# A four-layer attention and expert kernel: routing of the second mixture in one step, gate weights in the rows, loads ordered behind reads

## The chip, the core and the metric

One core of one Trainium2 chip runs the whole kernel: TensorE (matmuls and transposes), VectorE, ScalarE, GpSimd (here also the indirect DMAs) and the DMA queues, SP's above all. The metric is the device time in microseconds (us) of one execution, median of several runs.

## The reference, cut to what matters

The input is x of 4 batches x 512 tokens x 128 columns, and a context of 32 rows a batch. Four layers follow one another, each an attention over the context and a feed-forward part, both added to x. The change is in the feed-forward part of the third layer (layer index 2, "the second mixture": 8 experts, the two best for each token, 640 places per expert) and in the start of the fourth layer, whose feed-forward part is again a mixture of experts.

```python
def _moe_forward(x, w_g, c_fc, c_proj):
    ...
    logits = xf @ w_g
    topv, topi = jax.lax.top_k(logits, TOP_K)
    full = full.at[jnp.arange(N)[:, None], topi].set(topv)
    probs = jax.nn.softmax(full, axis=-1)
    ...
    rank = jnp.cumsum(mask.reshape(TOP_K * N, N_EXP), axis=0).reshape(TOP_K, N, N_EXP) - 1
    mask = mask * (rank < capacity)
    ...
    exp_batches = jnp.einsum('nec,nd->ecd', sec_mask, xf)
    h = jax.nn.gelu(jnp.einsum('ecd,edh->ech', exp_batches, c_fc), approximate=False)
    exp_out = jnp.einsum('ech,ehd->ecd', h, c_proj)
    out = jnp.einsum('nec,ecd->nd', cb, exp_out)
```

All first choices come before all second choices in an expert's count; a token whose rank is over the capacity is dropped there. With two choices the softmax weights are w1 = 1 / (1 + exp(m2 - m1)) for the larger logit m1, and w2 = w1 * exp(m2 - m1).

## The kernel before, in words

Tokens lie on 128 partitions; a batch is a tile X[g] of 128 x 4 x 128 f32, and all work is done batch by batch. Each batch's work is a Python generator, a chain; `together` traces the chains in turns, one step (up to the next `yield`) of each per turn, and chain g begins two turns after chain g - 1. The framework plans the order of instructions on each engine from that: what was traced earlier goes first among what it takes to be ready by its own costs, so that work of several batches is interleaved on an engine, but each engine then executes its queue strictly in this order and waits where an operand is late. Semaphores are set by the framework.

**Attention and normalisation.** `moments` makes the statistics (L203 to L216, with Ln and Exp on ScalarE at L208 and L209), `normed` the normalised tile (L230 on ScalarE or L234 on VectorE), `transposed` four TensorE transposes (L244) and a copy (L246). `psum(fill=5)` puts five matmuls of the identity on TensorE first (L93, "fillers"), whose results nobody reads. `attend` is the attention proper (L396 scores, L381 to L383 softmax, L409 transposes, L415 values), `proj` the projection (L256), `add_to` the addition to X (L468). `attend_few` is the attention with few keys of layers 1 and 2 (L441, L457, L463).

**Second mixture, routing.** After layer 2's attention, `routed` (tag 2) normalises into the tiles rows[g] (128 x 4 x 129: the row and the number of its token) and makes the logits (matmuls L575, copy L581). `dispatch.chain(g)` then has three steps. First the two best experts of each token (twice L633 to L639 on VectorE, with L642 between), and the counts per expert (matmul L649, copy to SBUF L651). Second the ranks: matmuls L654 to L657 with this and the earlier batches' counts, then L660 to L672 on VectorE, which end in `to`, the row of each choice in the DRAM table xs2; its tiles have two buffers (`own`). Third, 8 scatters (L680), each an indirect DMA issued by GpSimd that writes 128 rows; those of first choices wait for the landing of the earlier batches' second choices. `finish` makes `back` (L712), which marks the places of each expert that hold second choices, and the weights wt[0] and wt[1] for all tokens (L715 to L719). `l3_weights` (L319, L338 and others) prepares the next layer's keys after that.

**Second mixture, experts.** `l2_ffn` reads each expert's 640 rows (L1147, three experts ahead), and takes them in two groups, of 3 x 128 and of 2 x 128: transposes (L835), copy (L836), first product (L1171), Gelu on ScalarE (L1174), second product (L1179), copy of the results from PSUM (L1186), and a scatter per 128 results to the DRAM table yd2 (L1188); its row numbers are made per expert at L1164. `combine(g)` reads both results of each token of a batch (L1204, two reads of 256 KB) and adds them to X with their weights (L1210, eight operations per batch).

**Fourth layer.** Per batch: `combine2`, `attend3` (`normed`, `transposed` with 5 fillers, `attend`, GpSimd's addition of a bias at L1235, `proj`), `route3` (`routed` with 5 fillers). Beside these four chains a fifth, `fetch`, traces the loads of the last mixture's weights f3w1 and f3w2 (L1407, L1408; 1 MB each) from turn 8 on. Their tiles use the space of the second mixture's weights, and can be loaded when the last product that reads those is done. `l3_ffn` is the last mixture (L1253, L1254, L1301, L1311), which runs all experts for all tokens.

Reads, loads and the stores of the output are all on SP's queue.

Of the kernel before, what the change touches and what calls it, by code (L numbers as in the profile page):

```python
# [8 lines left out]
F32 = mybir.dt.float32  # L9
# [7 lines left out]
P = 128  # L17
D = 128
B = 4
# [52 lines left out]
def tile_kernel(ctx: ExitStack, tc: tile.TileContext, I, out):  # L72
# [489 lines left out]
    def routed(tag, w, bias=None, copies=(), fill=0, rows=None):  # L562
# [5 lines left out]
        def chain(g):  # L568
# [3 lines left out]
            xnT[g] = yield from transposed(xn[g], fill=fill)  # L572
# [35 lines left out]
    def dispatch(dp, C2, xs, cleared, rows, logits, wt):  # L608
# [9 lines left out]
        m = dp.tile([P, 2, NT], F32, tag="m", name="m")  # L618
# [4 lines left out]
        def own(cols, name, dtype=F32):  # L623
            return dp.tile([P] + cols, dtype, tag=name, name=name, bufs=2)

        def chain(g):
# [4 lines left out]
            w = own([2, n], "w")  # L631
            for k in range(2):
                nc.vector.tensor_reduce(m[:, k, ts], L, AX.X, ALU.max)  # L633
                at = own([n, NEXP], "at", BF16)
                nc.vector.tensor_tensor(at, L, bc(m[:, k, ts], 2, NEXP), ALU.is_equal)
# [9 lines left out]
            while len(counts) < g:  # L645
                yield
# [5 lines left out]
            yield  # L652
# [22 lines left out]
            yield  # L675
# [29 lines left out]
        def finish():  # L705
# [7 lines left out]

            d = dp.tile([P, NT], F32, tag="d", name="d")
            nc.vector.tensor_tensor(d, m[:, 1], m[:, 0], ALU.subtract)  # L715
            nc.scalar.activation(d, d, AF.Exp)
            nc.vector.tensor_scalar(wt[0], d, 1.0, None, ALU.add)
            nc.vector.reciprocal(wt[0], wt[0])
            nc.vector.tensor_tensor(wt[1], wt[0], d, ALU.mult)  # L719
            return back  # L720
# [412 lines left out]
    def l2_ffn(xs, yd, back, wt, f2w1, f2w2, meanwhile):  # L1133
        made = []

# [8 lines left out]
        def read(e):  # L1144

            xg.append(ex.tile([P, NCH2, D + 1], F32, tag="xg", name="xg", bufs=4))
            nc.sync.dma_start(xg[e], xs[e * L2_CAP : (e + 1) * L2_CAP].rearrange("(p c) d -> p c d", c=NCH2))  # L1147
# [10 lines left out]
        for i, (e, c0, m) in enumerate(groups):  # L1158
            if c0 == 0:
# [4 lines left out]
                nc.vector.scalar_tensor_tensor(to, back[:, e, :], float(NTOK), xg[e][:, :, D], ALU.mult, ALU.add)  # L1164
            if i + 1 < len(groups):
# [20 lines left out]
            nc.vector.tensor_copy(flat(y[:, :m, :]), pt[:, : m * D])  # L1186
# [11 lines left out]

        def combine(g):
            ys = []  # L1200
            for k, tag in enumerate(("o", "oT")):
                y = wk.tile([P, NJ, D], F32, tag=tag, name="yg", bufs=B)
                at = k * NTOK + g * S
                nc.sync.dma_start(y, yd[at : at + S].rearrange("(j p) d -> p j d", p=P))  # L1204
                ys.append(y)
            yield
            for j in range(NJ):
                for k in range(2):
                    xj = X[g][:, j, :]
                    nc.vector.scalar_tensor_tensor(  # L1210
# [412 lines left out]
```

## Time and profile before

| | us |
|---|---|
| timed, median of 3 runs | 660.22 (657.69 to 662.02) |
| profiled execution | 654.48 |
| its span, first to last instruction | 652.7 |
| TensorE busy | 533.0 (82% of the span) |
| VectorE busy | 330.6 (51%) |
| ScalarE busy | 238.9 (37%) |
| GpSimd busy | 152.6 (23%) |

From the page: the span in 40 slices of 16.3 us, each digit the busy share in tenths; PEclk is TensorE's granted clock in tenths of full speed, DMA the mean busy share of the 16 DMA engines.

```profile
PE   2569889735988888899663799991899999999996
...
DVE  4686554663278532789742211213877863233232
...
POOL 4243233335302102000476155541200000000000
PEclk9887999956989999999867799996699999999999
DMA  9960001221495009200011321018000000000000
```

Slices 19 to 22 (counted from 0; 310 to 375 us) hold the second mixture's routing and scatters: POOL is at 4 to 7 there, and TensorE falls to 3 before it. In slices 23 to 26 the experts run on a full TensorE. Slice 27 (440 to 457 us) is the gap between the second mixture's last product and the fourth layer: TensorE at 1, the DMA engines at 8. From slice 32 on the last mixture keeps TensorE full to the end. Busy time of an instruction is that of the instruction alone; overlapped matmuls count more than the time they take.

### The profile page before, as it was taken

What the parts mean: (1) busy time and instruction counts of PE and PEld (TensorE: products, weight loads), DVE (VectorE), ACT (ScalarE), POOL (GpSimd) and SP (SyncE); (2) the same over time, 40 slices, a digit from 0 to 9 for tenths busy, and PEclk for the clock granted to TensorE, in tenths of its full rate; (3) what the DMA queues carried; (4) which work ended last, traced back from release to release, by engine and by line L of the source; (5) the groups of instructions that cost most, each with busy time, mean ns of one, the idle gap of its engine ahead of it and who ended that gap; (6) DMA issues with size and microseconds to landing.
All of it is one profiled execution on the core that took longest, in us unless ns stands there. A gap on an engine that the chain in (4) does not pass through costs nothing.

```text
span 652.7 us, 9532 instructions
## 1 busy us (share of the span) xinstructions
PE 533.0 (82%) x3426; PEld 423.4 (65%) x3426; DVE 330.6 (51%) x1361; ACT 238.9 (37%) x539; POOL 152.6 (23%) x188
## 2 busy tenths in 40 slices
PE   2569889735988888899663799991899999999996
PEld 2558667525986655798541688880578866767664
DVE  4686554663278532789742211213877863233232
ACT  2353655411227621542210233340555343333432
POOL 4243233335302102000476155541200000000000
PEclk9887999956989999999867799996699999999999
DMA  9960001221495009200011321018000000000000
GB/s 321 312 210 17 18 17 50 64 81 38 158 305 211 1 1 314 81 2 2 29 49 53 106 78 61 32 34 271 3 0 2 1 1 2 17 0 17 7 11 17
DMA packets 41985, 48.84 MB, mean 75 GB/s; under 512 B 5129, under 2 KB 29074, under 8 KB 41762
## 3 DMA queue, kind: packets, MB, share of 16 engines
q1 hardware_dynamic: 38690, 40.56, 18.9%
q0 software_dynamic: 2816, 5.79, 2.7%
q10 hardware_dynamic: 432, 1.89, 0.8%
q8 instruction: 27, 0.44, 0.3%
q14 instruction: 20, 0.16, 0.1%
HBM read 37.72 MB, written 13.14 MB: 78 GB/s over the span
## 4 chain that ended last, share of the span: by engine, by line
PE 47%; POOL 8%; issue 7%; DMA 6%; DVE 5%; ACT 4%; SPq 1%; DVEq 0%; POOLq 0%; ACTq 0%
PE pt L1301 9%; PE pt L1253 9%; POOL yd L1188 6%; PE pt L93 5%; PE pt L396 3%; PE po L415 3%; PE pt L244 3%; PE pt L256 2%; DMA yd<-ye,to 2%; PE pt L1045 2%; PE pt L575 2%; DMA e_wg<-in_e_wg 1%; ACT xnT L246 1%; PE pt L409 1%; PE pt L983 1%
## 5 line engine op out<-in xcount | busy, mean ns | idle before, releaser
L1301 PEld LDWEIGHTS pt<-f3w,hT 128*128 128x128 f32 x512 | 65.3, 191 | 33.2 <-ACT hT L1254 19.4
L1311 DVE SCALAR_TENSOR_TENSOR x<-pt,gates,x 128x128 f32<-128x128 f32 x128 | 35.9, 344 | 76.6 <-PE pt L1301 76.5
L1254 ACT ACTIVATE hT<-pt,cols 128x512 f32<-128x512 f32 x64 | 44.0, 687 | 73.5 <-PE pt L1253 73.0
L1301 PE MATMUL pt<-f3w,hT 128*128 128x128 f32 x512 | 68.5, 277 | 1.0 <-ACT hT L1254 0.6
L1253 PE MATMUL pt<-xnT,f3w 128*128 128x512 f32 x128 | 65.1, 597 | 0.0
L93 PE MATMUL pt<-cst 128*128 128x128 f32 x392 | 55.4, 289 | 0.0
L93 PEld LDWEIGHTS pt<-cst 128*128 128x128 f32 x392 | 51.2, 204 | 2.8 <-issue 1.5
L1188 POOL DMA_INDIRECT yd<-ye,to x40 | 38.3, 957 | 48.8 <-DVE ye L1186 25.4
L680 POOL DMA_INDIRECT xs<-rows,to x32 | 31.0, 968 | 64.4 <-issue 61.0
L1174 ACT ACTIVATE hT<-pt 128x384 f32<-128x384 f32 (+1 forms) x64 | 27.6, 437 | 45.5 <-PE pt L1171 43.9
L246 ACT COPY xnT<-pt 128x512 f32<-128x512 f32 x40 | 23.4, 584 | 55.9 <-PE pt L244 55.6
L203 DVE BATCH_NORM_STATS2 st<-x 128x6 f32<-128x128 f32 x128 | 32.4, 271 | 22.0 <-POOL x L556 16.1
L1179 PEld LDWEIGHTS pt<-f2w,hT 128*128 128x128 f32 x320 | 39.6, 191 | 3.3
L1179 PE MATMUL pt<-f2w,hT 128*128 128x128 f32 x320 | 40.6, 279 | 0.0
L244 PE MATMUL pt<-cst,xn 128*128 128x128 f32 x80 | 18.2, 324 | 25.6 <-ACT xn L230 18.4
L1171 PE MATMUL pt<-exT,f2w 128*128 128x256 f32 (+1 forms) x128 | 38.9, 447 | 0.2 <-DVE exT L836 0.2
L1186 DVE COPY ye<-pt 128x384 f32<-128x384 f32 (+1 forms) x16 | 7.9, 491 | 51.8 <-PE pt L1179 51.8
L244 PEld LDWEIGHTS pt<-cst,xn 128*128 128x128 f32 x80 | 12.0, 159 | 32.2 <-ACT xn L230 21.2
L1171 PEld LDWEIGHTS pt<-exT,f2w 128*128 128x128 f32 x128 | 23.8, 197 | 8.9 <-issue 1.4
L381 DVE TENSOR_REDUCE mx<-pt 128x16 f32<-128x512 f32 (+1 forms) x32 | 22.0, 687 | 14.4 <-PE pt L396 13.9
L396 PE MATMUL pt<-keys,xnT 128*128 128x256 f32 (+1 forms) x64 | 27.6, 540 | 1.3 <-ACT xnT L246 1.3
L415 PEld LDWEIGHTS po<-v,aT 128*128 128x128 f32 x192 | 24.8, 199 | 4.9 <-issue 3.5
(330 smaller groups left out, 1053.5 us busy)
## 6 DMA issues: line engine op xcount, KB each, us to landing
e_w<-in_e_w SPq DMA_DIRECT2D x8, 512.0 KB, 6.4
e_wg<-in_e_wg SPq DMA_DIRECT2D x8, 512.0 KB, 6.8
yg<-yd SPq DMA_DIRECT2D x12, 256.0 KB, 4.2
xs<-in_empty SPq DMA_DIRECT2D x1, 2580.0 KB, 11.3
xg<-xs SPq DMA_DIRECT2D x8, 322.5 KB, 3.0
f0w<-in_f_w SPq DMA_DIRECT2D x1, 2048.0 KB, 13.5
yd<-zero SPq DMA_DIRECT2D x8, 256.0 KB, 3.7
ew<-in_e_w SPq DMA_DIRECT2D x8, 256.0 KB, 4.1
```

The source lines that it names most:

```text
L93: nc.tensor.matmul(pt[:, :P], lhsT=ident, rhs=ident, start=True, stop=True)
L203: nc.vector.bn_stats(st[:p, j, :], src[:, j, :])
L244: nc.tensor.transpose(pt[:, j * P : (j + 1) * P], src[:, j, :], ident)
L396: nc.tensor.matmul(pt[:, j * nk : (j + 1) * nk], lhsT=xT[:, (j0 + j) * P : (j0 + j + 1) * P], rhs=keys, start=True, stop=True,)
L415: nc.tensor.matmul(po[:, k, :], lhsT=aT[:, k * P : (k + 1) * P], rhs=of(values[k % nch], cols + hpc, g), start=True, stop=True,)
L1171: nc.tensor.matmul(pt[:, : m * P], lhsT=f2w1[:, e, f * P : (f + 1) * P], rhs=xT, start=True, stop=True)
L1179: nc.tensor.matmul(pt[:, c * D : (c + 1) * D], lhsT=hT[:, f, c * P : (c + 1) * P], rhs=f2w2[:, e, f, :], start=f == 0, stop=f == 3,)
L1188: ins = nc.gpsimd.indirect_dma_start(out=yd[:], out_offset=bass.IndirectOffsetOnAxis(ap=to[:, c0 + c : c0 + c + 1], axis=0), in_=y[:, c, : ...
L1253: nc.tensor.matmul(pt, lhsT=f3w1[:, e, f * P : (f + 1) * P], rhs=xnT[g], start=True, stop=True)
L1254: nc.scalar.activation(hT[:, f, :], pt, AF.Gelu, bias=col["f3_b1"][:, 2 * e + f : 2 * e + f + 1])
L1301: nc.tensor.matmul(pt[:, j, :], lhsT=hT[:, f, j * P : (j + 1) * P], rhs=f3w2[:, e, f, :], start=f == 0, stop=f == 1,)
L1311: nc.vector.scalar_tensor_tensor(xj, pt[:, j, :], ge, xj, ALU.mult, ALU.add)
```

## The change

The routing of the second mixture (`dispatch.chain`) becomes one step: the `yield`s after the counts and after the ranks go, and the waiting loop ahead of the counts becomes an assertion. Its small tiles get four buffers in place of two.

The weights are computed in that step per batch, between the counts and the ranks, and put into two more columns of the rows (128 x 4 x 131), so that they travel with the scatter; the DRAM table, the table of empty rows and the experts' input tiles are wider by two columns. `finish` loses the weights and makes `first` = 1 - `back` in addition. In `l2_ffn` three small operations per expert make `gate`, the weight that belongs to each place, and the copy of the results from PSUM becomes a multiplication by it. `combine` then adds two whole tiles per batch.

The fillers go from `route2` (all batches), from `attend3` (all but batch 0) and from `route3` (all but batch 3).

`fetch` waits (in tracing) until the combining reads of all batches are traced, and its two loads get a dependency on the landing of all eight reads.

```diff
@@ routed @@
-            xnT[g] = yield from transposed(xn[g], fill=fill)
+            xnT[g] = yield from transposed(xn[g], fill=fill[g] if isinstance(fill, tuple) else fill)
@@ dispatch @@
-        m = dp.tile([P, 2, NT], F32, tag="m", name="m")
...
         def own(cols, name, dtype=F32):
-            return dp.tile([P] + cols, dtype, tag=name, name=name, bufs=2)
+            return dp.tile([P] + cols, dtype, tag=name, name=name, bufs=B)
...
+            m = own([2, n], "m")
             for k in range(2):
-                nc.vector.tensor_reduce(m[:, k, ts], L, AX.X, ALU.max)
+                nc.vector.tensor_reduce(m[:, k], L, AX.X, ALU.max)
...
             nc.scalar.copy(ohs[:, 2], ohs[:, 0])
-            while len(counts) < g:
-                yield
+            assert len(counts) == g
...
             nc.scalar.copy(cs[: 2 * width], pt[: 2 * width, :P])
-            yield
+
+            d = own([n], "d")
+            nc.vector.tensor_tensor(d, m[:, 1], m[:, 0], ALU.subtract)
+            nc.scalar.activation(d, d, AF.Exp)
+            w1, w2 = rows[g][:, :, D + 1], rows[g][:, :, D + 2]
+            one = own([n], "one")
+            nc.vector.tensor_scalar(one, d, 1.0, None, ALU.add)
+            nc.vector.reciprocal(w1, one)
+            nc.vector.tensor_tensor(w2, w1, d, ALU.mult)
             pt = psum()[:, : 3 * width]
             nc.tensor.matmul(pt, lhsT=tri, rhs=flat3, start=True, stop=False)
...
                     to[:, k], at[:, k], float(NSLOT + (L2_CAP if k else -1)), over[:, k], ALU.add, ALU.max
                 )
-            yield
...
         def finish():
...
-            d = dp.tile([P, NT], F32, tag="d", name="d")
-            nc.vector.tensor_tensor(d, m[:, 1], m[:, 0], ALU.subtract)
-            nc.scalar.activation(d, d, AF.Exp)
-            nc.vector.tensor_scalar(wt[0], d, 1.0, None, ALU.add)
-            nc.vector.reciprocal(wt[0], wt[0])
-            nc.vector.tensor_tensor(wt[1], wt[0], d, ALU.mult)
-            return back
+            first = rk.tile([P, NEXP, NCH2], F32, tag="first", name="first")
+            nc.vector.tensor_scalar(first, back, -1.0, 1.0, ALU.mult, ALU.add)
+            return back, first
@@ l2_ffn @@
-            xg.append(ex.tile([P, NCH2, D + 1], F32, tag="xg", name="xg", bufs=4))
+            xg.append(ex.tile([P, NCH2, D + 3], F32, tag="xg", name="xg", bufs=4))
...
                 nc.vector.scalar_tensor_tensor(to, back[:, e, :], float(NTOK), xg[e][:, :, D], ALU.mult, ALU.add)
+
+                gate = ex.tile([P, NCH2, 2], F32, tag="gate", name="gate", bufs=4)
+                nc.vector.tensor_tensor(gate[:, :, 1], back[:, e, :], xg[e][:, :, D + 2], ALU.mult)
+                nc.vector.tensor_tensor(gate[:, :, 0], first[:, e, :], xg[e][:, :, D + 1], ALU.mult)
+                nc.vector.tensor_tensor(gate[:, :, 0], gate[:, :, 0], gate[:, :, 1], ALU.add)
...
-            nc.vector.tensor_copy(flat(y[:, :m, :]), pt[:, : m * D])
+            nc.vector.tensor_tensor(
+                y[:, :m, :], pt[:, : m * D].rearrange("p (c d) -> p c d", d=D), bc(gate[:, c0 : c0 + m, 0], 2, D), ALU.mult
+            )
...
+        combined = []
+
         def combine(g):
...
-                nc.sync.dma_start(y, yd[at : at + S].rearrange("(j p) d -> p j d", p=P))
+                combined.append(nc.sync.dma_start(y, yd[at : at + S].rearrange("(j p) d -> p j d", p=P)).ins)
                 ys.append(y)
             yield
-            for j in range(NJ):
-                for k in range(2):
-                    xj = X[g][:, j, :]
-                    nc.vector.scalar_tensor_tensor(
-                        xj, ys[k][:, j, :], wt[k][:, g * NJ + j : g * NJ + j + 1], xj, ALU.mult, ALU.add
-                    )
-            yield
+            for y in ys:
+                nc.vector.tensor_tensor(flat(X[g]), flat(y), flat(X[g]), ALU.add)
+            yield
@@ l3_xattn @@
-            xT = yield from transposed(x1, fill=5)
+            xT = yield from transposed(x1, fill=0 if g else 5)
@@ tile_kernel @@
-            route2, _, _, L = routed(2, wide["w_g"], None, (), 5, rows)
+            route2, _, _, L = routed(2, wide["w_g"], None, (), 0, rows)
...
-        route3, _, xnT, L = routed(3, wide["router"], fill=5)
+        route3, _, xnT, L = routed(3, wide["router"], fill=(0, 0, 0, 5))
...
             def fetch():
-                nc.sync.dma_start(f3w1, I["f3_w1"].rearrange("e d f -> d e f"))
-                nc.sync.dma_start(f3w2, I["f3_w2"].rearrange("e (c p) d -> p e c d", p=P))
+                while len(combined2) < 2 * B:
+                    yield
+                for load in (
+                    nc.sync.dma_start(f3w1, I["f3_w1"].rearrange("e d f -> d e f")).ins,
+                    nc.sync.dma_start(f3w2, I["f3_w2"].rearrange("e (c p) d -> p e c d", p=P)).ins,
+                ):
+                    for read in combined2:
+                        tc.add_manual_dep(
+                            load,
+                            read.name,
+                            mybir.DependencyInfo(mybir.DependencyClass.Sync, mybir.DependencyReason.DATA),
+                            reason="what is wanted now comes first",
+                        )
                 yield
```

More of the change, by code (lines that the diff above doesn't have):

```diff
@@ L606, in without, with dispatch @@
         return L2
-    def dispatch(dp, C2, xs, cleared, rows, logits, wt):
+    def dispatch(dp, C2, xs, cleared, rows, logits):
         same3, before3 = (dp.tile([P, 96], BF16, tag=n, name=n) for n in ("b_same3", "b_before3"))
@@ L631, in chain @@
             w = own([2, n], "w")
+            m = own([2, n], "m")
             for k in range(2):
-                nc.vector.tensor_reduce(m[:, k, ts], L, AX.X, ALU.max)
+                nc.vector.tensor_reduce(m[:, k], L, AX.X, ALU.max)
                 at = own([n, NEXP], "at", BF16)
-                nc.vector.tensor_tensor(at, L, bc(m[:, k, ts], 2, NEXP), ALU.is_equal)
+                nc.vector.tensor_tensor(at, L, bc(m[:, k], 2, NEXP), ALU.is_equal)
                 nc.vector.tensor_tensor(at, at, bc(rev, 1, n), ALU.mult)
@@ L1130, in l2_xattn, with l2_ffn @@
         return chain
-    def l2_ffn(xs, yd, back, wt, f2w1, f2w2, meanwhile):
+    def l2_ffn(xs, yd, back, f2w1, f2w2, meanwhile):
         made = []
+        back, first = back
         def ready(steps):
@@ L1203, in combine @@
                 at = k * NTOK + g * S
-                nc.sync.dma_start(y, yd[at : at + S].rearrange("(j p) d -> p j d", p=P))
+                combined.append(nc.sync.dma_start(y, yd[at : at + S].rearrange("(j p) d -> p j d", p=P)).ins)
                 ys.append(y)
             yield
-            for j in range(NJ):
-                for k in range(2):
-                    xj = X[g][:, j, :]
-                    nc.vector.scalar_tensor_tensor(
-                        xj, ys[k][:, j, :], wt[k][:, g * NJ + j : g * NJ + j + 1], xj, ALU.mult, ALU.add
-                    )
+            for y in ys:
+                nc.vector.tensor_tensor(flat(X[g]), flat(y), flat(X[g]), ALU.add)
             yield
-        return combine, made[0]
+        return combine, combined, made[0]
     def l3_weights():
@@ L1323, in tile_kernel @@
     yd2 = dram.tile([2 * NTOK + NEXP * L2_CAP, D], F32, tag="yd2", name="yd2")
-    xs2 = dram.tile([SPARE + 2 * NTOK, D + 1], F32, tag="xs2", name="xs2")
+    xs2 = dram.tile([SPARE + 2 * NTOK, D + 3], F32, tag="xs2", name="xs2")
     zero = wk.tile([P, NJ, D], F32, tag="oT", name="zero", bufs=B)
@@ L1375, in tile_kernel @@
         attend1, attend2 = l1_xattn(*made["few1"]), l2_xattn(*made["few2"])
-        wt = [rk.tile([P, NT], F32, tag=f"wt{k}", name=f"wt{k}") for k in range(2)]
         dp_scope = ExitStack()
@@ L1382, in l2_start @@
             C2 = packed("cst2", _CST2, pool=dp)
-            rows = [dp.tile([P, NJ, D + 1], F32, tag=f"rows{g}", name="rows") for g in range(B)]
-            route2, _, _, L = routed(2, wide["w_g"], None, (), 5, rows)
-            send, finish = dispatch(dp, C2, xs2, cleared2, rows, L, wt)
+            rows = [dp.tile([P, NJ, D + 3], F32, tag=f"rows{g}", name="rows") for g in range(B)]
+            route2, _, _, L = routed(2, wide["w_g"], None, (), 0, rows)
+            send, finish = dispatch(dp, C2, xs2, cleared2, rows, L)
             sent.append(finish)
@@ L1398, in tile_kernel @@
         with tc.tile_pool(name="ex2", bufs=1) as ex:
-            combine2, many3 = l2_ffn(xs2, yd2, back2, wt, f2w1, f2w2, l3_weights)
+            combine2, combined2, many3 = l2_ffn(xs2, yd2, back2, f2w1, f2w2, l3_weights)
         attend3 = l3_xattn(*many3)
@@ L1487, in _empty_slots @@
     import numpy as np
-    t = np.zeros((NSLOT, D + 1), np.float32)
+    t = np.zeros((NSLOT, D + 3), np.float32)
     t[:, D] = NTOK + np.arange(NSLOT)
```

## The prediction

> **What bounds the kernel now.** I read the page's slices first, then the chain of waits, then the timelines of the stretches that the change touches, and last the busy times in windows. The second mixture's routing, its experts and the results' way into the third stage lie between 300 and 525 us; before and after them the diff changes nothing but a table that is 1.6% larger.
>
> The timeline of GpSimd (start, duration, engine, line, operation, then in brackets the idle time before):
>
> ```profile
> 261.41 0.62 POOL L266 TENSOR_TENSOR keys<-kc,cst 128x256 f32<-128x256 f32 x1 [0.17 <-PE pt L1099]
> 316.95 1.02 POOL L680 DMA_INDIRECT xs<-rows,to  x1 [54.93 <-issue]
> 318.28 0.96 POOL L680 DMA_INDIRECT xs<-rows,to  x1 [0.30 <-DVE logits L642]
> ...
> 355.17 0.96 POOL L680 DMA_INDIRECT xs<-rows,to  x1 [0.30 <-issue]
> 356.44 0.96 POOL L680 DMA_INDIRECT xs<-rows,to  x1 [0.30 <-issue]
> ```
>
> From 316.95 the 32 scatters run back to back, 1.264 us apart: 40.45 us. GpSimd is the bound there, and only the start of the first scatter can move the end. Its timeline, all engines, shows what the first one waits for:
>
> ```profile
> 310.73 0.24 PE L649 MATMUL pt<-b_ones,ohs 128*64 128x128 bf16 x1 [2.29 <-DVE ohs L639]
> 310.90 1.42 PE L93 MATMUL pt<-cst 128*128 128x128 f32 x10
> 311.01 0.26 ACT L651 CAST cs<-pt 64x128 bf16<-64x128 f32 x1
> ...
> 314.67 0.29 PE L654 MATMUL pt<-ohs,b_tri 128*128 128x96 bf16 x1
> ...
> 316.04 0.24 DVE L672 SCALAR_TENSOR_TENSOR to<-row,over 128x4 int32<-128x4 f32 x2
> ```
>
> Batch 0's counts are in SBUF at 311.27, but its rank product (load at 314.46) stands behind other batches' matmuls, five fillers (L93) among them.
>
> From 363.5 to 441.2 TensorE is busy 77.64 of 77.7 us: the experts are TensorE-bound. Then the chain of waits (start, length):
>
> ```profile
> 443.53 4.99 DMA yd<-ye,to
> 448.54 2.61 DMA yg<-yd
> 452.23 1.13 DVE x L1210 x4
> 457.60 1.65 PE pt L244 x4
> 459.90 2.08 PE pt L396 x2
> 461.98 2.13 PE pt L93 x10
> ```
>
> The last scatter takes 4.99 us to land, where the median is 2.2. The two f3w loads are issued at 439.38 and 441.29 and take 5.4 and 7.1 us: all 16 DMA engines are at 0.86 to 0.93 from 440 to 448. Busy times by stretch (length, then PE, PEld, DVE, ACT, POOL, clock):
>
> ```profile
> 457.60:468.50 10.90, 9.02 (x26) 5.91 (x27) 10.21 (x45) 5.72 (x15) 2.76 (x2) 0.50 0.00 0
> 468.50:508.40 39.90, 39.14 (x258) 30.53 (x257) 29.80 (x83) 22.34 (x45) 2.54 (x2) 0.99 0.01 1
> 508.40:525.40 17.00, 15.28 (x127) 14.05 (x126) 12.44 (x63) 6.46 (x15) 0.00 (x0) 1.00 0.00 0
> ```
>
> First VectorE is full, with TensorE at half clock; then TensorE is full; in the tail both are nearly so.
>
> **Part 1, the routing.** With the three steps in one, the rank product is traced ahead of the other batches' steps, so it can follow the counts: 314.46 - 311.27 = 3.2 us less. On GpSimd the scatters pass nothing, for it idles from 262 to 317. The filler of batch 0 (chain: 303.53, 1.12 us) is in front of all this on a full TensorE: 1.1 us less. Added ahead of the scatter are d, Exp, one, reciprocal and w2: nearest rows L715 to L719 (0.22, 0.21, 0.18, 0.25, 0.17, on 16 columns, here 4), 1.0 us if all in line, nothing if they fit the 0.6 us in which the counts go to ScalarE and back. I take 0.4, since Exp is queued behind the counts' copy on ScalarE and VectorE, in order, then waits for it; behind that wait are batch 0's ranks and batch 1's normalisation. That normalisation (L234, 1.11 us) is traced earlier, and may push in between: 0 to 1.1, I take 0.4. First scatter: 3.2 + 1.1 - 0.8 = 3.5 us earlier (1.1 if the matmuls in between stay, 4.3 if all additions hide), at 313.4. Batch 1's index must then be there at 313.4 + 10.1 - 0.7 = 322.8. It was ready at 323.67, behind two fillers (1.12 and 1.34) and a late L654, so about 321: GpSimd is not starved, with 2 us to spare; batches 2 and 3 (331.86 and 339.43) have over 1 and 3 us even unmoved. Everything to 443.5 moves by 3.5. Four index buffers for two remove VectorE's 1.17 us wait at L672; GpSimd ends last anyway, so nothing. Rows of 524 instead of 516 bytes: 1.6% of a 2.80 us read, 0.04 us; of the 11.3 us table copy 0.2 us, unused until 317.
>
> **Part 2, the experts.** Eight times three gate operations of 0.17 us (L1164's row) are 4.1 us on VectorE, busy 14.5 of 77.7 us; TensorE's queue covers them. Uncovered they would cost those 4.1. At expert 0 they fall in the 0.76 us in which VectorE waits for the transposes. The eviction turns from a copy (558 ns for 384 columns) into a product with a broadcast operand: L382's row, 688 ns for 512, gives 516. Nothing. The finish loses five small operations and gains one (L712: 0.19), all under the scatters.
>
> **Part 3, the last loads behind the results.** Without the loads the last scatter should land in the usual 2.2 to 2.3 us: 4.99 - 2.3 = 2.7 us less (0 if its lateness is its own, 2.8 at best). The loads then go out on SP's queue once the eighth read has landed, some 9 us after the first read's issue. 2 MB at the 300 GB/s of this stretch is 7 us; L1253 needs them 74 us after that issue. The slack is over 50 us; only the stores of the output are behind them on SP, at the end of the kernel.
>
> **Part 4, the third stage's start.** Combining takes two 128x512 additions (674 ns each, the row of the first mixture's addition) for eight of 342 ns. For batch 0: 1.35 against 451.17 to 453.36, so 0.8 us. In all VectorE has 10.7 - 8 x 0.674 = 5.3 us less. In the first stretch TensorE's idle time (1.9) and a filler (2.3) could both go: 0 to 4.2; I take 1.8, for the first attention block also waits on ScalarE and on GpSimd's additions (L1235). Fillers of batches 2 and 3 lie in the full stretch: 2 x 1.12 = 2.2. Of the three removed at 508.4, 513.9 and 518.2, the second stands before a transpose whose input is ready (1.1), the first before one that comes 0.2 us later anyway, the third under VectorE's work for batch 3: 1.2 (0.2 to 2.2). Sum 0.8 + 1.8 + 2.2 + 1.2 = 6.0 (1.6 to 9.4).
>
> **A row and a rule.** TensorE restarts twice from half clock: at 362.0 the clock is full after 4.7 us of unbroken work, at 457.6 only after 11.5, with 1.2 us of idling at 465 in between; it also fell at 312 after 2.3 us of idling. The fillers are TensorE activity. "TensorE: Matmul & The Clock Gate" of the Trainium skill (Part 1) says that about 3.4 us of sustained work raises the clock, and that the windows run freely; the first restart comes near to that, the second does not. By the rule, leaving fillers out can postpone the rise by one window, and half of it, 1.7 us, would come off the sum below.
>
> **Sum.** 3.5 + 2.7 + 6.0 = 12.2 us. The profiled execution took 654.48 us (span 652.7, 1.8 around it), so it would take 642.3. The timed runs lie higher (657.69 to 662.02, median 660.22); from that median it is 648.0.
>
> **Rivals.** *Late clock.* The two restarts differ by 11.5 - 4.7 = 6.8 us: so much a missed rise costs. Without the filler at 462 it is missed once more; at half clock half of that, 3.4 us, is lost: 651.4. For it: the idle 1.2 us at 465 and the 0.50. Against it: VectorE frees TensorE's inputs earlier, so real work takes the fillers' place.
>
> *Fillers were free.* They ran while TensorE waited for a normalisation, and the routing gains only its one filler: 1.1 + 2.7 + 0.8 + 1.0 = 5.6, 654.6. For it: the third and half the first of the tail's fillers do so. Against it: 39.14 of 39.9 us busy.
>
> *GpSimd starved* (the new wait in place of the old). VectorE stands still at Exp while the other batches' work queues behind it, and the index tiles come more than 10.1 us apart. Until now they come 7.4, 8.2 and 7.6 us apart; at 13 us apart the scatters end 3 x 2.9 = 8.7 us later, and the gain shrinks to 3.5: 656.7. From 10.1 + 12.2/3 = 14.2 us on it is no gain at all.
>
> *Slower: the clock falls in the full stretch.* From 468.5 to 508.4, 39 us of full-speed TensorE work; each us of it done at half clock costs another. From 12.2 us on the gain is gone; with half the stretch, 19.5 - 12.2 = 7.3 us are lost: 667.5. For it: the fall at 312. Against it: from 476 to 508 there is no filler now, and TensorE is busy 3.65 us or more of every 4 at clock 1.00.
>
> **Chances.** Forecast 0.55, better than its bounds 0.04, late clock 0.15, free fillers 0.15, starved 0.06, clock fall 0.05. This kernel's measurement can tell about 1%, 6.6 us, from no change: faster below 653.6, slower above 666.8. The forecast, the better case, nearly all of the late clock and a fifth of the free fillers are faster: 0.76. Slower are the clock fall and a third of the starved case: 0.07; 0.17 remain. The range goes from 642 (15.5 us gained, and 2.5 us of the median's own scatter) to 656 (free fillers, with a little scatter): it leaves out the clock fall, the starved case, and edges.
>
> **What would show it.** The first scatter at about 313.4 and the 32nd 39.2 us after it; a gap over 0.30 among them says starved. The last yd scatter landing in 2.3 us, f3w issued after the yg reads. TensorE's stretch from its restart to the third stage's first L1253 about 62 us where it was 67.7, its clock full no more than 11 us after the restart. If routing's L654 still comes 3 us after the counts, part 1 was wrong; if idle time takes the place of the L93 rows, part 4.

## The result and the profile after

The changed kernel takes 652.41 us (median of four runs, 650.83 to 654.4), the kernel before 661.09 us beside it (657.69 to 662.02). The ratio is 0.988, 95% interval 0.9831 to 0.9928. The medians differ by 8.7 us, the interval says 4.8 to 11.2, and 12.2 were forecast.

The profiled executions don't show it. After's took 654.40 us with a span of 652.6, before's 654.48 with 652.7. The first question is therefore which of the two is unlike the timed runs. In the page of after, first the span, then five rows of the 40 slices of 16.3 us:

```profile
span 652.6 us, 9344 instructions
...
PE   2568988736988887998625699993799799999996
...
DVE  4787545663288532789534322113777763233232
...
POOL 4333233235302102000657055452200000000000
PEclk9878999956989999999657699998599999999999
DMA  8960001221495009100111321014300000000000
```

Slices 19 to 22 (the routing) have a clock of 6, 5, 7, 6 where it was 8, 6, 7, 7. In slice 27 the DMA engines are at 4 instead of 8 and in slice 28 at 3 instead of 0: the last loads have moved behind the results. TensorE is at 7 in slice 31, ahead of the last mixture, where it was at 9.

GpSimd's timeline (start, duration, engine, line, operation, idle time before it). The scatters are at L686 now:

```profile
312.85 1.02 POOL L686 DMA_INDIRECT xs<-rows,to  x1 [51.86 <-issue]
314.17 0.97 POOL L686 DMA_INDIRECT xs<-rows,to  x1 [0.31 <-issue]
...
331.87 0.96 POOL L686 DMA_INDIRECT xs<-rows,to  x1 [0.30 <-issue]
338.09 0.96 POOL L686 DMA_INDIRECT xs<-rows,to  x1 [5.26 <-issue]
```

The first scatter comes at 312.85, 4.1 us earlier. But the 17th, batch 2's first, waits 5.26 us, and the 32nd ends at 358.80 where it ended at 357.40.

The chain of waits (start, length), and after it SP's own timeline:

```profile
446.89 2.23 DMA yd<-ye,to
449.13 0.37 SPq L1215
449.55 3.08 DMA yg<-yd
452.72 0.70 DVE x L1219
```

```profile
449.13 5.29 SPq L1215 DMA_DIRECT2D yg<-yd  x8
458.42 0.37 SPq L1416 DMA_DIRECT2D f3w<-in_f_w  x1
459.01 0.71 SPq L1417 DMA_DIRECT2D f3w<-in_f_w  x1
```

The last yd scatter lands in 2.23 us, not 4.99, and the loads go out at 458.42. The last stage's stretch, by windows (length, then busy time of PE, PEld, DVE, ACT, POOL with counts, clock, DMA share, GB/s):

```profile
458.31:470.50 12.19, 10.16 (x27) 5.70 (x28) 9.32 (x39) 7.43 (x21) 3.79 (x3) 0.50 0.48 172
470.50:508.40 37.90, 36.43 (x232) 27.71 (x231) 29.16 (x80) 20.91 (x39) 1.27 (x1) 0.99 0.00 1
508.40:525.16 16.76, 13.39 (x91) 11.83 (x90) 10.77 (x57) 6.06 (x14) 0.00 (x0) 0.90 0.00 1
```

From TensorE's restart at 458.31 to the last mixture's first product (L1260) at 525.16 are 66.85 us where 67.67 were. TensorE's busy time there fell from 63.4 to 60.0 us; idle time took most of what the fillers left. And the clock, 1.00 in the tail of before, is 0.90 in it.

### The profile page after: what moved, and what is told of

Read it like the earlier page. It is cut to its first block, busy times and chain, and to the rows that moved or that the text cites. A ratio compares the mean times of both kernels' runs of the same rounds, so it can differ in the third digit from the quotient of the medians.

```text
span 652.6 us, 9344 instructions
## 1 busy us (share of the span) xinstructions
PE 525.4 (81%) x3326; PEld 411.9 (63%) x3326; DVE 331.1 (51%) x1374; ACT 239.5 (37%) x542; POOL 153.2 (23%) x188
## 4 chain that ended last, share of the span: by engine, by line
PE 36%; issue 23%; POOL 7%; DVE 4%; ACT 3%; DMA 3%; SPq 0%; DVEq 0%; POOLq 0%; ACTq 0%; another core or an unknown queue 0%
PE pt L1308 9%; PE pt L1260 9%; POOL yd L1197 6%; PE pt L93 2%; PE pt L244 2%; PE po L415 2%; PE pt L1046 2%; PE pt L396 2%; PE pt L984 1%; DMA yd<-ye,to 1%; PE pt L256 1%; ACT xnT L246 1%; PE pt L1178 1%; PE pt L998 1%; DMA yg<-yd 1%
## 5 line engine op out<-in xcount | busy, mean ns | idle before, releaser
L1260 PE MATMUL pt<-xnT,f3w 128*128 128x512 f32 x128 | 65.1, 597 | 0.0
L686 POOL DMA_INDIRECT xs<-rows,to x32 | 31.5, 986 | 66.3 <-issue 65.3
L93 PE MATMUL pt<-cst 128*128 128x128 f32 x292 | 40.8, 286 | 0.0
L244 PE MATMUL pt<-cst,xn 128*128 128x128 f32 x80 | 19.6, 336 | 25.3 <-ACT xn L230 15.8
L93 PEld LDWEIGHTS pt<-cst 128*128 128x128 f32 x292 | 37.9, 202 | 1.5 <-issue 1.0
L1193 DVE TENSOR_TENSOR ye<-pt,gate 128x384 f32<-128x384 f32 (+1 forms) x16 | 7.9, 491 | 52.4 <-PE pt L1186 52.4
L244 PEld LDWEIGHTS pt<-cst,xn 128*128 128x128 f32 x80 | 12.1, 159 | 34.4 <-ACT xn L230 20.6
```

What stands on the lines that cost most here:

```text
L93: nc.tensor.matmul(pt[:, :P], lhsT=ident, rhs=ident, start=True, stop=True)
L244: nc.tensor.transpose(pt[:, j * P : (j + 1) * P], src[:, j, :], ident)
L1260: nc.tensor.matmul(pt, lhsT=f3w1[:, e, f * P : (f + 1) * P], rhs=xnT[g], start=True, stop=True)
```

## The experiments

The runs were made on three chips, A, B and C. Ratios are to the kernel before on the same chip, which took 660.8 us on A, 653.2 on B and 660.6 on C.

| run | chip | us, median | ratio | 95% interval |
|---|---|---|---|---|
| before_again | A | 660.87 | 1.0004 | 0.9988 to 1.002 |
| after_again | A | 651.85 | 0.9865 | 0.984 to 0.989 |
| loads_only | A | 656.51 | 0.9941 | 0.9921 to 0.996 |
| onestep_only | A | 660.51 | 0.9996 | 0.9982 to 1.001 |
| nofill_only | B | 656.09 | 1.0037 | 1.0026 to 1.0048 |
| weights_only | B | 651.53 | 0.9966 | 0.9952 to 0.9981 |
| after_yields | B | 649.34 | 0.9943 | 0.9926 to 0.9961 |
| after_fill3 | B | 644.79 | 0.9862 | 0.9837 to 0.9887 |
| after_same_chip | C | 652.53 | 0.9888 | 0.985 to 0.9927 |
| after_fill3_again | C | 651.87 | 0.9896 | 0.9849 to 0.9944 |
| onestep_again | C | 659.42 | 1.001 | 0.9972 to 1.0049 |
| after_fills | C | 655.22 | 0.9923 | 0.9894 to 0.9953 |

What the same places in all 14 profiled executions show (us; "scatter" is the routing's, and a wait is GpSimd's idle time of over 0.45 us ahead of one; "half clock" is what of the last column but one ran at clock 0.50):

| execution | span | batch 0's counts | first scatter | waits | 32nd ends | last yd scatter to the read | read to restart | clock full after the restart | restart to the last mixture | half clock |
|---|---|---|---|---|---|---|---|---|---|---|
| before | 652.7 | 310.73 | 316.95 | none | 357.40 | 5.01 | 9.06 | 11.5 | 67.67 | 11.5 |
| before_again (A) | 659.1 | 310.54 | 316.78 | 4.79 | 361.81 | 5.47 | 9.07 | 11.8 | 67.79 | 11.8 |
| loads_only (A) | 654.7 | 310.69 | 317.15 | 4.68 | 362.53 | 2.24 | 9.18 | 7.9 | 66.36 | 7.9 |
| onestep_only (A) | 658.6 | 310.74 | 313.52 | 0.49, 8.72, 0.87 | 363.87 | 5.13 | 9.56 | 7.6 | 66.36 | 7.6 |
| onestep_again (C) | 657.4 | 311.98 | 315.14 | 2.61, 4.94 | 363.23 | 5.21 | 9.07 | 8.0 | 66.37 | 8.0 |
| nofill_only (B) | 655.8 | 311.64 | 316.85 | none | 357.89 | 5.19 | 9.09 | 11.8 | 69.62 | 15.3 |
| weights_only (B) | 650.7 | 311.23 | 317.45 | none | 357.93 | 5.11 | 9.50 | 7.5 | 64.55 | 7.5 |
| after | 652.6 | 309.42 | 312.85 | 5.26 | 358.80 | 2.24 | 9.18 | 13.1 | 66.85 | 16.5 |
| after_again (A) | 651.5 | 309.90 | 313.32 | 3.82 | 357.87 | 2.25 | 9.72 | 11.1 | 66.85 | 18.0 |
| after_same_chip (C) | 648.9 | 309.03 | 312.45 | 4.62 | 357.77 | 2.23 | 9.74 | 10.5 | 64.55 | 10.5 |
| after_yields (B) | 646.1 | 309.42 | 315.71 | none | 357.02 | 2.24 | 9.20 | 10.4 | 64.48 | 10.4 |
| after_fill3 (B) | 645.2 | 311.13 | 314.56 | none | 355.34 | 2.25 | 9.88 | 6.3 | 64.48 | 6.3 |
| after_fill3_again (C) | 646.7 | 309.17 | 312.28 | 3.69 | 356.72 | 2.24 | 9.81 | 5.9 | 64.50 | 5.9 |
| after_fills (C) | 655.4 | 310.67 | 313.45 | 0.91, 8.54, 0.98 | 363.99 | 2.24 | 9.77 | 5.4 | 64.48 | 5.4 |

From the last mixture's first product to the end every execution takes 127.4 us. Of before and after, the two first profiles, the chip isn't known.

**Both kernels again.** No edit.

> The kernel before, once more. Its first profile took 654.5 us, its timed runs 657.7 to 662.0. Theory 1 (the first profile was a lucky execution): the new profile shows 657 us or more, and somewhere between 300 and 525 us some 3 to 7 us of waiting that the first did not have. Rival (profiles and timed runs differ as such): again 654 to 655 us with the scatters back to back for 40.5 us.

> The changed kernel, once more. Its profile showed GpSimd waiting 5.3 us before batch 2's scatters. Theory 1 (the gap belongs to that execution): no gap over 1 us among the 32 scatters, the first at 312 to 314 us, the 32nd at 352 to 354, the time 649 to 651 us. Rival (the gap belongs to the one-step routing's order): again a gap of 4 us or more at the same scatter, the 32nd at 357 or later.

The kernel before, profiled again, has a span of 659.1 and waits ahead of batch 2's scatters as after does:

```profile
335.81 0.96 POOL L680 DMA_INDIRECT xs<-rows,to  x1 [0.30 <-issue]
341.56 0.95 POOL L680 DMA_INDIRECT xs<-rows,to  x1 [4.79 <-issue]
```

So the waits that the first theory of before_again asked for are there, and of after_again the rival holds (its gap is 3.82 us, a little under the 4 named): before's first profile was the unusual one. That it was a lucky execution is not shown. Its chip isn't known, and its 654.48 us would be an ordinary time on a chip like B, where the kernel before took 651.72 to 654.53. Against before_again, after_again ends the 32nd scatter 3.9 us earlier, gains 3.2 at the last yd scatter and 0.9 from the restart to the last mixture, loses 0.65 between the read and the restart, and ends 7.6 us earlier; the timed medians differ by 9.0.

**The last loads alone.** The kernel before with `combined`, the waiting loop and the dependencies of `fetch`:

```diff
+                while len(combined2) < 2 * B:
+                    yield
                 for load in (
...
+                    for read in combined2:
+                        tc.add_manual_dep(load, read.name, ...)
```

> The kernel before with the last loads ordered behind the combining reads, and nothing else. Theory 1 (the loads delay the last scatter): the last scatter to the results' table lands in 2.2 to 2.3 us instead of 5.0, the time falls by 2.7 us (ratio 0.996). Rival (the reads then pay for it, or the lateness is the scatter's own): time unchanged within 1 us.

The first theory holds: the scatter lands 3.2 us earlier (5.47 to 2.24). The time falls by more, 4.3 us. The clock is full 7.9 us after the restart here where it was 11.8, and the stretch is 1.4 us shorter; that part is not the loads' own work, since the stretch is just as long in both executions of the single step, where the loads are early.

**The single routing step alone.** Twice, on A and on C:

```diff
-            while len(counts) < g:
-                yield
+            assert len(counts) == g
...
             nc.scalar.copy(cs[: 2 * width], pt[: 2 * width, :P])
-            yield
...
-            yield
```

> The kernel before with the routing of the second mixture in one step and four buffers instead of two; fillers, weights and loads as before. Theory 1: the rank product follows the counts, the first scatter starts 2.5 to 3.2 us earlier relative to the counts' matmul, the 32 scatters stay back to back, and the time falls by 2.5 to 3.2 us (ratio 0.995 to 0.996). Rival (starved): a gap of several us at batch 2 or 3, and the time does not fall.

> The kernel before with the single routing step alone, again. Theory 1 (the late starts decide): on a chip whose scatters of the kernel before run without a gap, 3 to 3.5 us faster than the kernel before, the 32nd scatter ending near 354; on a chip with the gap, no change, as in the first run of it. Theory 2 (the order itself makes the gap ahead of batch 2): a gap of 4 us or more and no gain on any chip.

Nothing gained, twice. From batch 0's counts to the first scatter it takes 2.8 and 3.2 us instead of 6.2, and yet the 32nd scatter ends 2.1 us later than in before_again on A. On C, where the kernel before has no profile, it ends 51.3 us after the counts, as in before_again. The rival of onestep_only foretold the gap and that the time does not fall. What GpSimd waits for is seen in the timeline of onestep_only (all engines but GpSimd):

```profile
322.19 1.06 PE L244 MATMUL pt<-cst,rows 128*128 128x128 f32 x4
...
333.35 0.58 ACT L246 COPY xnT<-pt 128x512 f32<-128x512 f32 x1 [12.02 <-remote]
...
333.99 2.08 PE L575 MATMUL pt<-w,xnT 128*128 128x128 f32 x8 [10.73 <-issue]
336.18 0.19 DVE L581 COPY logits<-pt 128x32 f32<-128x32 f32 x1 [11.93 <-PE pt L575]
```

Batch 2's transposes (L244) are over at 323.25. ScalarE has nothing else to do and waits for nothing but them, and starts the eviction at 333.35. The trace's record of the semaphore that L244 raises stands at 333.33: the release itself came 10 us late. TensorE and VectorE then stand idle behind it. In after, VectorE shows the same in smaller pieces:

```profile
329.24 0.17 DVE L636 TENSOR_TENSOR at<-at,b_rev 128x32 bf16<-128x32 bf16 x1 [0.25 <-issue]
332.03 0.18 DVE L637 TENSOR_REDUCE w<-at 128x4 f32<-128x32 bf16 x1 [2.62 <-remote]
332.13 0.16 DVE L657 TENSOR_SCALAR one<-d 128x4 f32<-128x4 f32 x1
333.43 0.19 DVE L639 TENSOR_TENSOR ohs<-at,w 128x32 bf16<-128x32 bf16 x1 [1.14 <-DVE one L657]
```

L637 reads what L636 wrote at 329.41, on the same engine, and starts 2.6 us later. Engines that wait for one semaphore, and idle on for over 1 us after the last instruction that raises it has ended, are found only between 322 and 361 us, while the scatters run and just behind them. It is so in all eight executions on A and C and in after; the late results are TensorE's and VectorE's. Several of these waits last 1.2 us (1.22, 1.25, 1.21 and 1.23 in after_same_chip), near the 1.26 us from one scatter to the next. In the four executions on B and in before's first profile there is none, and GpSimd never waits over 0.45 us.

The same nine traces lack records of semaphore updates: VectorE has 1228 to 1234 instructions that raise its semaphore and 1176 to 1189 records. In the other five traces every such instruction of the three engines has its record within 0.35 us of its end. Records are lacking or late only from 154 to 170 and from 315 to 450 us, while GpSimd issues indirect DMAs. A lacking record is not by itself a late release: the counts' matmul ends at 320.34 in onestep_only without one, and ScalarE copies its result at 320.38. So the recording is disturbed in the executions with late releases; whether one causes the other, or a third thing both, no run separates.

Here batch 2's first scatter on B (after_fill3, GpSimd's timeline):

```profile
333.60 0.96 POOL L686 DMA_INDIRECT xs<-rows,to  x1 [0.30 <-DVE m L633]
334.86 0.96 POOL L686 DMA_INDIRECT xs<-rows,to  x1 [0.30 <-issue]
```

That the page "Perfetto Trace Analysis" of the Trainium skill (Tensor Engine Instruction) calls TensorE's end an estimate from the instruction's size leaves open whether L244 ended late or its signal came late; VectorE's own L636 in after, whose end it doesn't call one, speaks for the signal. Theory 1 of onestep_again asked for a chip without late releases; C wasn't one, and the single step alone was not tried on B. Its second theory (a gap ahead of batch 2 on any chip) is refuted for the single step within the change, by after_fill3 on B; its gap on C also stood ahead of batches 1 and 3, not of batch 2.

**The fillers alone.**

```diff
-        routed(2, wide["w_g"], None, (), 5, rows)
+        routed(2, wide["w_g"], None, (), 0, rows)
...
-            xT = yield from transposed(x1, fill=5)
+            xT = yield from transposed(x1, fill=0 if g else 5)
...
-        routed(3, wide["router"], fill=5)
+        routed(3, wide["router"], fill=(0, 0, 0, 5))
```

> The kernel before with one edit: the fillers go from the second mixture's routing, from attention for batches 1 to 3 and from the last routing for batches 0 to 2, as in the change. Theory 1 (the fillers were free: idle time and half clock take their place): 659.5 to 661.5 us, the same as before; from TensorE's restart to the first product of the last mixture 67 to 68 us, where the kernel before has 67.7 and 67.8; the first scatter about 1 us earlier, and a wait ahead of batch 2's scatters that eats it. Theory 2 (the prediction's): 1.1 us in the routing, 2.2 in the full stretch and 1.2 in the tail go: 656 to 657 us, and the stretch after the restart falls to 64 to 64.5 us. Theory 3 (the clock): the half-clock stretch after the restart grows by a window of 3.4 us, and the time by 1 to 3 us.

2.9 us slower, so the third theory. By windows, restart to last mixture:

```profile
458.74:470.60 11.86, 8.69 (x20) 4.25 (x21) 10.75 (x47) 7.40 (x19) 2.52 (x2) 0.50 0.00 0
470.60:509.50 38.90, 36.12 (x220) 27.12 (x220) 27.52 (x78) 20.96 (x41) 2.54 (x2) 0.96 0.00 1
509.50:528.36 18.86, 14.55 (x110) 12.52 (x109) 13.99 (x67) 6.79 (x16) 0.00 (x0) 1.00 0.00 1
```

TensorE has 4.1 us less to do (59.4 against 63.4) and takes 1.9 us longer (69.62): its clock rises as late as before and falls for another 3.4 us in the full stretch (0.96).

**The weights with the rows alone.** `gate`, the multiplication by it and the two additions per batch, with three steps, fillers and early loads (and four buffers for the routing's small tiles, as in the change):

```diff
+            gate = ex.tile([P, NCH2, 2], F32, tag="gate", name="gate", bufs=4)
...
-                    nc.vector.scalar_tensor_tensor(xj, ys[k][:, j, :], wt[k][:, ...], xj, ALU.mult, ALU.add)
+                nc.vector.tensor_tensor(flat(X[g]), flat(y), flat(X[g]), ALU.add)
```

> The kernel before with one edit: the weights travel with the rows, so that each expert's results are multiplied by its gate and combining is two additions per batch; three routing steps, fillers and the order of the last loads stay as before. Theory 1: VectorE's saving in combining does not reach the end, since from the reads of the results to TensorE's restart it takes 9.1 us in the kernel before and 9.2 to 9.7 in the changed one: 660 to 661.5 us. Theory 2 (the prediction's part 4): combining gives 0.8 us ahead of the restart and up to 1.8 in the first stretch behind it: 658 to 659 us. Theory 3: the small operations that leave the end of the routing take the wait ahead of batch 2's scatters (4.8 us) with them: 656 to 657 us, with no gap over 1 us among the scatters.

1.65 us faster by the medians, 1.2 to 3.1 by the interval: the second theory's size (1.8 to 2.8). The place is not the combining: from the read to the restart it takes 9.50 us. It is the stretch behind it, 64.55 where the kernel before has 67.7 (clock full after 11.5 to 11.8 us) and 66.4 where its clock rises as early as here (loads_only and both single steps). So VectorE's saving is worth 1.8 us at an equal clock, all of it won by batch 0's projection (L256, 43.27 us after the restart in loads_only, 41.47 here); the other 1.3 go with the clock. Theory 3's gap could not decide: B shows none without the edit either.

**The change with one part undone.** First the routing in three steps again:

```diff
-            assert len(counts) == g
+            while len(counts) < g:
+                yield
```

> The changed kernel with one part undone: the routing is three steps again (the weights are still made with them and sent with the rows). Theory 1: the single step is worth its 3.5 us once the rest of the change is there, because the wait ahead of batch 2's scatters is no longer than before: 655 to 656 us, the first scatter at 316 to 317, the 32nd ending near 361.5. Theory 2: the wait ahead of batch 2's scatters is what ends the routing, and the first scatter's time does not matter: 651.5 to 652.5 us, with a wait of 0 to 1.5 us ahead of batch 2 and the 32nd ending near 358.

Then the fillers behind the restart back (`fill=5` in `attend3` and `route3`):

```diff
-            xT = yield from transposed(x1, fill=0 if g else 5)
+            xT = yield from transposed(x1, fill=5)
```

> The changed kernel with one part undone: the fillers of attention and of the last routing are back, those of the second routing stay out. Theory 1 (they were free): 651.5 to 652.5 us, and from the restart to the first product of the last mixture 66 to 67.3 us, where the changed kernel has 66.85. Theory 2 (the prediction's): they cost what they last, 3.4 to 5 us: 655 to 657 us and 70 to 72 us. Theory 3 (they hold the clock up): no fall of the clock in the tail at 516 to 524 and an earlier rise after the restart: 649.5 to 651 us, and 64.5 to 66 us.

> The changed kernel unchanged, to stand beside the versions that are compared with it on one chip. Theory 1 (the whole change is worth the same 1.2 to 1.4% on any chip): ratio to the kernel before 0.986 to 0.989. Theory 2 (the late starts while the scatters land belong to some chips, and without them the single step gives its 3.5 us as well): no gap over 1 us among the scatters, the first at 313 and the 32nd ending near 353.5, the ratio 0.984 to 0.988 where the fallen clock in the tail takes its 2 to 3 us. If instead the chip shows the gap, the 32nd ends near 358.

> The changed kernel with the fillers of attention and of the last routing back, again, beside the changed kernel on one chip. Theory 1 (the fillers hold the clock up; without them it rises one window later or falls in the tail): 2 to 4 us faster than the changed kernel, from the restart to the last mixture's first product 64.5 us against 66.85, and no half-clock window between 475 and the end. Theory 2 (the 64.48 us were chance, since the changed kernel without the single step had 64.48 without those fillers too): within 1 us of the changed kernel. Theory 3 (the prediction's): 3 to 5 us slower.

And all fillers back, the routing's too:

> The changed kernel with all fillers back, those of the second routing too. Theory 1 (only the fillers behind the restart matter): as fast as the version with those of attention and the last routing, or up to 1.1 us slower, since the filler of batch 0 is again ahead of the first scatter (at 314 to 315). Theory 2 (the fillers of the routing hold up the clock there as well): 1 to 2 us faster than that version, with fewer half-clock windows between 312 and 345.

The absolute figures of the first two expectations belong to A; B's kernel before takes 7.6 us less, so ratios decide. On B, from the counts to the end of the 32nd scatter it takes 46.3 (nofill_only), 46.7 (weights_only) and 47.6 us (after_yields) with three steps and 44.2 (after_fill3) with one: where no release is late, the single step is worth 2.0 to 3.4 us, counted from the counts. The theories of after_yields both lean on the wait ahead of batch 2, which B does not show, and are not decided. No execution of the changed kernel was made on B, so its two versions stand beside each other alone: 649.34 and 644.79.

The fillers behind the restart: on C the changed kernel and the one with them are equal (652.53 and 651.87, intervals that overlap), as theory 2 of after_fill3_again said. The ratio of after_same_chip, 0.9888, is that of its theory 1, and the gap is there. On B, after_fill3 shows what its theory 3 named: a stretch of 64.48 us and no fall of the clock. The windows of after_fill3_again:

```profile
454.77:460.70 5.93, 5.25 (x15) 3.32 (x16) 5.93 (x29) 3.97 (x12) 1.48 (x2) 0.50 0.78 260
460.70:505.00 44.30, 43.48 (x291) 33.92 (x290) 34.44 (x96) 25.28 (x51) 3.60 (x3) 1.00 0.04 13
505.00:519.27 14.27, 12.55 (x104) 11.62 (x104) 9.85 (x51) 5.39 (x14) 0.00 (x0) 1.00 0.00 1
```

In the versions with the two additions the clock is full 5.4 to 7.5 us after the restart with fillers, 10.4 to 13.1 without them. (In those with the eight operations it took 7.6 to 11.8 even with fillers.) And yet the stretch takes 64.5 us both ways, as long as the clock then stays up. The starts of the batches' logits (first L575 of each batch, in us from the restart) tell where the time goes:

| execution | clock full | batch 0 | batch 1 | batch 2 | batch 3 | last mixture |
|---|---|---|---|---|---|---|
| before_again | 11.8 | 53.67 | 58.85 | 63.12 | 66.79 | 67.79 |
| loads_only | 7.9 | 52.25 | 57.42 | 61.70 | 65.37 | 66.36 |
| after | 13.1 | 51.26 | 55.32 | 60.85 | 65.86 | 66.85 |
| after_again | 11.1 | 50.38 | 54.44 | 60.13 | 65.86 | 66.85 |
| after_same_chip | 10.5 | 50.09 | 54.16 | 59.70 | 63.56 | 64.55 |
| after_fill3_again | 5.9 | 50.38 | 55.55 | 59.83 | 63.50 | 64.50 |

A late rise does cost. The first two rows differ in no TensorE work of this stretch: a rise 3.9 us later goes with 1.4 us at every batch. After and after_same_chip are one kernel: 2.5 us later, and 1.2 us at batches 0 to 2. That is 0.36 to 0.47 us for each us. The rise of after_same_chip is 4.6 us later than that of after_fill3_again, yet its batch 0 is not late. So leaving the fillers out gains something in the full stretch, and the late rise takes it back: at those rates at most 1.7 to 2.2 us, an estimate (a rise at 6.3 us in after_fill3 for 7.5 in weights_only brought only 0.1). In the tail the missing filler puts batch 1 1.4 us ahead; at batch 2 that is gone, for TensorE then stands idle for xn (1.20 us, below).

The clock did not stay up in two of the three executions of the changed kernel: 66.85. The tail on TensorE in after, and the same instructions in after_same_chip:

```profile
517.49 1.00 PE L244 MATMUL pt<-cst,xn 128*128 128x128 f32 x4 [1.20 <-DVE xn L234]
519.17 2.08 PE L575 MATMUL pt<-w,xnT 128*128 128x128 f32 x8 [0.68 <-ACT xnT L246]
521.04 2.02 PE L93 MATMUL pt<-cst 128*128 128x128 f32 x10
522.89 0.60 PE L244 MATMUL pt<-cst,xn 128*128 128x128 f32 x4
```

```profile
514.93 1.01 PE L244 MATMUL pt<-cst,xn 128*128 128x128 f32 x4 [1.20 <-DVE xn L234]
516.61 1.16 PE L575 MATMUL pt<-w,xnT 128*128 128x128 f32 x8 [0.68 <-ACT xnT L246]
517.61 1.28 PE L93 MATMUL pt<-cst 128*128 128x128 f32 x10
518.73 1.07 PE L244 MATMUL pt<-cst,xn 128*128 128x128 f32 x4
```

The idle pieces are the same, 1.20 and 0.68 us; in after the clock is at 0.50 from 519.2 to 522.6. By the clock's records, which change every 3.41 us or a multiple of it, one window of after, 515.8 to 519.2, holds both pieces; in after_same_chip a border at 515.3 lies between them. That is not the whole rule. In after_again, too, a border lies between them, at 516.1, and there the clock fell, until 523.0:

```profile
515.52 1.16 PE L244 MATMUL pt<-cst,xn 128*128 128x128 f32 x4 [1.20 <-DVE xn L234]
517.35 2.07 PE L575 MATMUL pt<-w,xnT 128*128 128x128 f32 x8 [0.67 <-ACT xnT L246]
```

What decides stays open. In after the fall costs 1.1 us: of the 2.3 us by which batch 3 is later than in after_same_chip, 1.2 stand at batch 2 already, ahead of the fall. In after_again it costs 2.0, of 2.3.

The routing's fillers are another matter. Where releases come late, the single step with them ends the 32nd scatter at 363.2 to 364.0 (three executions), without them at 356.7 to 358.8 (four). The kernel with all fillers takes 655.22 us on C by the median, 3.4 more than the one with only the later ones; theory 1 gave at most 1.1, and theory 2 is wrong in sign. The intervals of the two ratios overlap, so it is the profiles that show it (363.99 and 356.72). Why ten filler matmuls (0.5 and 1.2 us in onestep_only) go with 6 us is not shown; the fillers stand ahead of the transposes whose release is the late one.

## Why the prediction was right, and where not

The time is within the range and the sign is right; 8.7 us came of 12.2. By its parts:

*The base.* Right to take the difference off the timed median and not off the profile. But "from 316.95 the 32 scatters run back to back" was true of that execution alone: on A it loses 4.7 to 4.8 us there, and that is most of what lies between 654.48 and the median.

*Part 1, 3.5 us.* The first scatter: as forecast. Its lead on the counts fell from 6.2 to 3.1 to 3.4 us in the changed kernel and its versions without routing fillers, and it came at 312.3 to 313.3 on A, C and in after (313.4 forecast). "GpSimd is not starved, with 2 us to spare" failed: on A and C the wait ahead of batch 2 is 3.7 to 5.3 us, and up to 8.7 with fillers. That is the starved rival's wait, with another cause than it named: VectorE was not standing at Exp, releases came late. The gain of 3.9 us (361.81 to 357.87) is near the forecast, and that is luck: the single step, which was to bring most of it, is worth nothing alone on A and C. There the gain came only where the fillers went too. Whether their going is enough is not shown: three steps without fillers were run on B alone, where no release is late, and there the 32nd scatter ends at 357.89 without them and at 357.93 with them (weights_only).

*Part 2, nothing.* From TensorE's first transpose of the experts' rows to the last yd scatter it takes 81.4 us in weights_only against 81.5 in before; 81.0 to 83.0 in the versions of the changed kernel. Right, within 1.5 us.

*Part 3, 2.7 us.* 2.8 to 3.2 in the profiles, and the loads at 458.42 are hidden.

*Part 4, 6.0 us.* This is the term that failed; 0.3 us came in place of it on A and 2.6 on C (read to the last mixture: 76.57 and 74.29 against 76.86 in before_again; that is A's, and C has no profile of the kernel before). Its pieces:

Combining, 0.8: nothing. VectorE in after, and in before, between batch 0's statistics and the step that they feed:

```profile
454.45 0.68 DVE L1219 TENSOR_TENSOR x<-yg,x 128x512 f32<-128x512 f32 x1
...
455.24 0.69 DVE L1219 TENSOR_TENSOR x<-yg,x 128x512 f32<-128x512 f32 x1
455.85 0.16 DVE L206 TENSOR_SCALAR v<-mv 128x4 f32<-128x4 f32 x1
```

```profile
454.27 0.32 DVE L1210 SCALAR_TENSOR_TENSOR x<-yg,wt,x 128x128 f32<-128x128 f32 x1
...
454.60 0.31 DVE L1210 SCALAR_TENSOR_TENSOR x<-yg,wt,x 128x128 f32<-128x128 f32 x1
454.84 0.16 DVE L206 TENSOR_SCALAR v<-mv 128x4 f32<-128x4 f32 x1
```

Batch 0's own additions take 1.51 us for 2.19. But batch 1's stand between its statistics and its v (L206), two of them in either kernel, and they are twice as long now: 0.74 us back. The prediction counted the additions ahead of batch 0 and not those queued between its own steps.

The first stretch, 1.8: right in size, as weights_only shows at an equal clock.

The fillers, 2.2 and 1.2: this is the step that failed. They brought nothing net: 64.55 us without them, 64.50 with them. "Fillers lie in the full stretch" read TensorE's 39.14 busy of 39.9 us as a bound, though fillers are counted in it, and the sum left out the later rise, which the text had named as a rival. In the full stretch a gain was there, but the clock rose 4.6 us later and took it back: the late-clock rival. In the tail idle time took their place: the rival "Fillers were free". TensorE's waits there (for xnT from ScalarE, for xn from VectorE) point to the chain of one batch, which no run took apart. The measured 652.4 lies between the forecast's 648.0 and the 654.6 of that rival.

*The clock.* The late-clock rival reckoned that half of a later rise is lost; 0.36 to 0.47 of it was. A fall costs another 1.1 us in after and 2.0 in after_again; in nofill_only a fall goes with a stretch 1.9 us longer than before's. The rival of a falling clock had the right mechanism, one or two windows instead of half the stretch. The Trainium skill's page "TensorE: Matmul & The Clock Gate" (Part 1) has windows of 3413 ns that run freely. The traces agree: every change of the clock lies a multiple of 3.41 us from the next. The same page of the Trainium skill has 3.4 us of sustained work for the rise. These traces neither bear that out nor refute it: the 14 restarts took 5.4 to 13.1 us, and TensorE was busy for 73 to 91% of that time.

## What to carry to other kernels

A busy engine is a bound only after its fillers are taken off, and taking them out has its price: idle time takes their place where they stand in a chain of waits, and the clock may rise later or fall. When one profiled execution is faster than all timed runs, profile the kernel again before pricing slack from it: a gap that it lacks may be what the typical run pays. And of an operation made fewer but longer, price also what is queued between the steps of the work that it was to speed up.

## What the runs showed of the hardware

While indirect scatters follow each other at 1.26 us, an instruction's release can reach its waiter 1 to 10 us after the instruction ended (2.6 us in after, 10.1 in onestep_only), across engines and from an engine to itself. It was so on two of three chips and in none of B's four profiled executions, and the kernel before is 7.5 us faster on B. The traces with late releases also lack records of semaphore updates, the others don't. What delays the releases stays open: none of the instructions shown here waits on a DMA, no run held the scatters back to see it go, and none tells the recording's own part.

After a restart, a clock that rose 2.5 us later cost the same work 1.2 us (after beside after_same_chip), and one that rose 3.9 us later 1.4 us (before_again beside loads_only).
